# Four GNN layers on one core: two of four column blocks turned by VectorE, and a drain for the last pairs of the first three layers

## The chip, the cores and the metric

One core of a Trainium2 chip runs the whole program in one launch. The metric is the device time in microseconds. Everything is fp32.

## The reference, cut to what matters

There are 32 batches of 512 nodes with 64 features and one 512 x 512 adjacency matrix. Four layers are applied, each to `relu(layernorm(x))` and added to `x`:

```python
x = x + (h @ Ws + adj @ h @ Wn + bias)                      # layer 0
x = x + relu(adj @ relu(adj @ h @ W0) @ W1)                 # layer 1
x = x + elu(gat(h))                                         # layer 2: masked softmax attention
def gat_layer(x, graph, W, b):                              # layer 3
    h = x @ W
    s = einsum('bnd,bmd->bnm', h, h) * graph
    s = where(s == 0.0, -1e16, s)
    return einsum('bnm,bmd->bnd', softmax(s, axis=2), h) + b
cat = leaky_relu(concat of 8 heads of gat_layer, 0.01)
x = x + leaky_relu(gat_layer(cat, graph, W_out, b_out), 0.01)
```

Layer 3 has 8 heads per batch and one output layer per batch, so 9 x 32 softmaxes of 512 x 512.

## The kernel before, in words

The order of the work on PE (TensorE), DVE (VectorE) and ACT (ScalarE) is written out by hand: both stages run inside a manual schedule, in which those three engines take their instructions in program order. The queues of SP and POOL, which issue the DMAs, are ordered by the scheduler.

**Stage 1, layers 0 to 2.** The batches go in 16 pairs (M = 16). `slot(k, more)` (L1020) is one step of a software pipeline: in step k pair k is in layer 0, pair k-1 in the layer norm before layer 1, pair k-2 in the first half of layer 1, pair k-3 in its second half (`project(..., "po1b")`, L1051), pair k-4 in the preparation of layer 2 (`Gat.flip`, `prepare`, `weigh`) and pair k-5 in its scores, values and end (`Gat.scores`, L954: eight score products a pair on VectorE, L958; `values`, L963: 128 matmuls, L971; `end`, L978: the division by the sums, the exponential for elu, the two additions to x, and the centring for the next layer norm). The loop runs 21 steps, k = 0 to 20 (L1147), so that the last five steps have fewer and fewer pairs in them. Step 19 also takes the last pair's scores and values (L1103). `more` is a piece of set-up work for one step: `judge_rows(c)` (L193), six VectorE operations on one block of rows of the adjacency matrix, comes in steps 16 to 19, `judge` (L220), which gathers their verdict, in step 20. After step 17 the first steps of the attention pipeline, which have no scores yet, are put in (`flow_slot`, L1151): they make the normalized input of the first batch (`hn`, `hs`, `hx`).

**Stage 2, layer 3.** The work is cut into 144 units: 128 of two heads of one batch (`Heads`) and 16 of the output layer of two batches (`Out`). Each unit has C = 4 blocks of 128 rows, and a new unit begins every four slots of `planned` (L690). In its slots 0 to 3 a unit's scores for one block of rows (r) are reduced by VectorE and exponentiated by ScalarE: `scores` (L387, issued on PE one slot earlier into one of two PSUM buffers), `soft` (L363: on VectorE the masked row maximum, L378, for each of the two heads; on ScalarE the exponential, L371). The scores of slot k can be issued only when the buffer of two slots before has been read.

The weighted sum needs the probabilities transposed, in four blocks of 128 columns (j = 0 to 3), called column blocks below.
- Blocks 0, 1 and 2 take `transpose(j)` (L422), in slots 5, 6 and 7: 16 transposes of 64 x 64 on PE into two PSUM tiles, and two copies to SBUF. Both copies are on ScalarE (L436, L438), but for j = 1 the second is on VectorE (L441), after that slot's reductions.
- Block 3 takes `turn(r)` (L397) and `route` (L411). In slots 2 to 5, after that slot's reductions, VectorE transposes 32 x 32 blocks of the last 128 columns of both heads (L401, 128 x 256). After every second one POOL issues a write of 256 KB to a tile in DRAM (L406). In slot 5 `route` issues four reads of 128 KB (L415), two on SP, two on POOL, that put the blocks into the tile `turned`, of which there are two buffers.

`values(j)` (L443) multiplies in slots 6 to 9, one column block a slot, in PE's queue in order: block 3 in two halves of the columns, because of the order in which `turned` holds them. In slot 5 `recips` (L458) takes the reciprocals of the sums, writes them to DRAM by four small DMAs (L468, `rec_row`) and reads them back spread over the partitions by two (L473, `recb`), all six on SP. In slot 9 `normalize` (L480) multiplies by `recb` on VectorE; then follow the product with the head's weights (L565, `y_ps`), its bias on ScalarE and the leaky relu on VectorE. During eight slots of each nine units, the `Out` products (L604, `gT_ps`) are also on PE. A slot is called led when it begins with such a weight product; in a led slot the transposes come after the other PE work.

Of the kernel before, what the change touches and what calls it, by code (L numbers as in the profile page):

```python
# [8 lines left out]
F32 = mybir.dt.float32  # L9
AF = mybir.ActivationFunctionType  # L10
OP = mybir.AluOpType
# [11 lines left out]
def fast_form(  # L23
# [32 lines left out]
    Q = P // 32  # L56

# [256 lines left out]
    class Pair:  # L314
# [82 lines left out]
        def turn(self, r):  # L397
            if r == 0:
                self.turns = wk.tile([P, Q, C // 2, 2, 2, 32], F32, name="turn")
                self.rows = dram.tile([P, Q, C // 2, P], F32, name="turn_row")  # L400
            nc.vector.transpose(  # L401
                self.turns[:, :, r // 2, :, r % 2].rearrange("p a k i -> p k a i"),
                self.p[:, :, r, N - P :].rearrange("p k (a i) -> p k a i", i=32),
            )
            if r % 2:
                nc.gpsimd.dma_start(  # L406
                    self.rows[:, :, r // 2],
                    self.turns[:, :, r // 2].rearrange("p a k r i -> p a (k r i)"),
                )

        def route(self):  # L411
            rows = self.rows.rearrange("(b i) a g x -> a i b (g x)", b=Q)
            pt = wk.tile([P, Q, C // 2, 2, 2, 32], F32, name="turned")
            for a in range(Q):
                (nc.sync if a % 2 else nc.gpsimd).dma_start(  # L415
                    pt[a * 32 : (a + 1) * 32].rearrange("p b g k r i -> p b (g k r i)"), rows[a]
                )
            self.pts[C - 1] = [
                pt[:, :, :, k].rearrange("p b g r i -> p g r b i") for k in range(2)
            ]  # L420

        def transpose(self, j):  # L422
# [14 lines left out]
            if j != 1:  # L437
                nc.scalar.copy(pth[:, :, :, 1, :], ps[1])  # L438
                return None

            return lambda: nc.vector.tensor_copy(pth[:, :, :, 1, :], ps[1])  # L441

        def values(self, j):  # L443
# [3 lines left out]
            for k in range(2):  # L447

                parts = 2 if j == C - 1 and len(pt[k].shape) > 2 else 1
# [240 lines left out]
    def planned(units, products):  # L690
# [15 lines left out]
        def slot(k):  # L706
# [12 lines left out]
            copies = []  # L719

            def transposes():
                for u, j in at(k, TR, C - 1):
                    copies.append(u.transpose(j))
# [32 lines left out]
            for copy in copies:  # L756
                if copy:
                    copy()
# [43 lines left out]
    with (  # L802
# [105 lines left out]
        class Gat:  # L908
# [54 lines left out]
            def values(self):  # L963

                self.acc = [
                    ps_g.tile([P, C, F + 1], F32, name="acc") for k in range(2)
                ]
                for r in range(C):
# [9 lines left out]
            def end(self):  # L978
                rec = tiny.tile([P, 2, C], F32, name="rec")
                self.sq = o = work.tile([P, 2, C, F], F32, name="o")  # L980
                for k in range(2):
# [4 lines left out]
                    )  # L986
                e = row_pair("e")[:, 0].rearrange("p (k c f) -> p k c f", k=2, c=C)
# [31 lines left out]

        def slot(k, more):  # L1020
# [28 lines left out]
            if k - 3 in nt1b:  # L1049

                po = project([(nt1b.pop(k - 3), wl2[1])], "po1b")  # L1051
                x4 = pair_of(k - 3)
                for i in range(2):
                    nc.vector.scalar_tensor_tensor(
                        x4[:, i], po[:, :, i, :], 0.0, x4[:, i], op0=OP.max, op1=OP.add
                    )
# [14 lines left out]
            if l1:  # L1071
                po = project([(nt1, wl2[0])], "po1a")
                z = work.tile([P, C, F2], F32, name="z")
                nc.scalar.activation(z, po.rearrange("p c b f -> p c (b f)"), AF.Relu)
# [27 lines left out]

            last = gat.pop(M - 1) if k - 4 == M - 1 else None  # L1103
            if last:
                last.scores(0)
                last.scores(1)
# [631 lines left out]
```

## Time and profile before

| what | us |
|---|---|
| median of three runs (2257.47 to 2261.6) | 2259.0 |
| the profiled execution | 2259.57 |
| its span, first to last instruction | 2257.6 |
| PE busy | 2167.4 |
| DVE busy | 1748.1 |
| ACT busy | 1634.1 |
| POOL busy | 399.4 |
| the first scores of stage 2 begin | 455.96 |

Busy times are of the whole span; the two stages are different, so the shares of each are read from a table by windows. Matmul instructions overlap, so the time that PE needs for a group is the distance from its start to the start of the next group, not the length that its row shows. One fp32 matmul of the program shows as two instructions. In a timeline row the columns are start, length, engine, line, operation, tiles and count, and in brackets how long the engine had been idle and what ended that.

### The profile page before, as it was taken

Reading aid. Unit: us, or ns where it says so; the run is one execution under the profiler, and the core shown is the slowest. Engines: PE = TensorE matmul, PEld = TensorE weight load, DVE = VectorE, ACT = ScalarE, POOL = GpSimd, SP = SyncE. Lnnn points to the kernel's source line nnn. Section 1 sums busy time; section 2 is a strip of 40 time slices with the busy share of each in tenths; the row PEclk is TensorE's granted clock in tenths of the full one; section 3 lists DMA queues with packets and bytes.
Section 4 is the critical chain, followed back from the end, with each engine's and each line's share of the span. In section 5 each row is a group of like instructions: output and inputs, shape, how many; then the busy total and the mean of one; then the engine's idle time right before and its main releaser. Section 6 shows DMA issues by size and latency. Waiting matters only on the chain.

```text
span 2257.6 us, 47717 instructions
## 1 busy us (share of the span) xinstructions
PE 2167.4 (96%) x17338; PEld 1028.7 (46%) x17338; DVE 1748.1 (77%) x4542; ACT 1634.1 (72%) x3818; POOL 399.4 (18%) x616
## 2 busy tenths in 40 slices
PE   7999999789999999999999999999999999999997
PEld 4677666634444444444444434344444444444443
DVE  6788888777777787878787777777878787878785
ACT  3444443288888888888888888787878787878785
POOL 2000000012221212222222212222212122112221
PEclk9999999699999999999999999999999999999999
DMA  4000000023333333333333333333333333333333
GB/s 129 1 1 1 1 1 1 1 88 110 104 116 106 118 105 112 108 110 112 109 109 113 109 109 113 104 113 104 114 108 111 106 118 102 110 99 114 101 116 105
DMA packets 122979, 204.03 MB, mean 90 GB/s; under 512 B 29752, under 2 KB 76000, under 8 KB 122608
## 3 DMA queue, kind: packets, MB, share of 16 engines
q0 software_dynamic: 37376, 113.49, 16.5%
q1 hardware_dynamic: 85360, 87.42, 13.0%
q8 instruction: 139, 2.28, 0.4%
q14 instruction: 104, 0.85, 0.1%
HBM read 119.48 MB, written 80.28 MB: 88 GB/s over the span
## 4 chain that ended last, share of the span: by engine, by line
PE 59%; DVE 16%; issue 3%; DMA 1%; ACT 1%; SPq 0%; POOL 0%; DVEq 0%; POOLq 0%; ACTq 0%
PE s_ps L392 19%; PE av L452 18%; PE pt_ps L430 8%; DVE s_att L378 8%; PE y_ps L565 5%; PE gT_ps L604 5%; DVE pt_att L441 3%; PE g_ps L547 2%; DVE hs L518 1%; DVE turn L401 1%; DVE cat L312 1%; DVE hn L514 1%; DVE hn L513 0%; DVE least L522 0%; DVE least_out L625 0%
## 5 line engine op out<-in xcount | busy, mean ns | idle before, releaser
L371 ACT ACTIVATE p_att<-s_att,negmax 128x512 f32<-128x512 f32 x1152 | 827.0, 726 | 1.8 <-DVE negmax L378 0.8
L378 DVE CUSTOM_DVE_ANT_0 s_att<-s_ps,flow_neg 128x512 f32<-128x512 f32 x1152 | 736.4, 675 | 2.9 <-PE s_ps L392 2.9
L392 PE MATMUL s_ps<-hx,g 64*128 64x512 f32 x2048 | 573.1, 637 | 26.7 <-DVE negmax L378 23.1
L452 PE MATMUL av<-pt_att,hn 128*64 128x512 f32 x1536 | 414.2, 618 | 0.4 <-DVE rec L463 0.4
L406 POOL DMA_DIRECT2D turn_row<-turn x288 | 206.3, 716 | 1167.7 <-DVE turn L401 972.8
L430 PEld LDWEIGHTS pt_ps<-ident,p_att 64*128 64x128 f32 x6912 | 279.6, 138 | 280.6 <-issue 180.0
L436 ACT COPY pt_att<-pt_ps 128x512 f32<-128x512 f32 x432 | 250.6, 580 | 90.4 <-PE pt_ps L430 88.7
L430 PE MATMUL pt_ps<-ident,p_att 64*128 64x64 f32 x6912 | 312.6, 226 | 1.3 <-ACT pt_att L436 0.6
L392 PEld LDWEIGHTS s_ps<-hx,g 64*128 64x128 f32 x2048 | 155.7, 186 | 283.7 <-DVE negmax L378 132.0
L401 DVE STREAM_TRANSPOSE turn<-p_att 128x256 f32<-128x256 f32 x576 | 253.8, 441 | 18.1 <-ACT p_att L371 17.6
L573 ACT ACTIVATE cat<-y_ps,bh 128x512 f32<-128x512 f32 x256 | 162.0, 684 | 130.1 <-PE y_ps L565 130.1
L482 DVE TENSOR_TENSOR o_att<-av,recb 128x512 f32<-128x512 f32 x144 | 99.5, 691 | 189.2 <-PE av L452 182.7
L441 DVE COPY pt_att<-pt_ps 128x512 f32<-128x512 f32 x144 | 99.0, 687 | 180.9 <-PE pt_ps L430 180.9
L415 POOL DMA_DIRECT2D turned<-turn_row x288 | 163.1, 573 | 388.5 <-DMA turn_row<-turn 206.6
L371 ACT ACTIVATION_READ_ACCUMULATOR p_att<-s_att,negmax 128x1 f32 x1152 | 229.6, 199 | 0.0
L438 ACT COPY pt_att<-pt_ps 128x512 f32<-128x512 f32 x288 | 171.5, 596 | 0.0
L452 PEld LDWEIGHTS av<-pt_att,hn 128*64 128x64 f32 x1536 | 76.0, 134 | 194.2 <-issue 81.9
L312 DVE SCALAR_TENSOR_TENSOR cat<-cat 128x1024 f32<-128x1024 f32 x128 | 151.3, 1182 | 0.0
L452 PE MATMUL av<-turned,hn 128*64 128x256 f32 x1024 | 139.6, 392 | 0.0
L559 ACT COPY g<-g_ps 128x512 f32<-128x512 f32 x128 | 68.7, 589 | 91.5 <-PE g_ps L547 91.5
L565 PE MATMUL y_ps<-o_att,wh_sb 64*128 64x512 f32 x512 | 132.5, 594 | 0.0
L604 PE MATMUL gT_ps<-cat,wo_sb 128*64 128x512 f32 x512 | 131.9, 592 | 0.0
(174 smaller groups left out, 2148.0 us busy)
## 6 DMA issues: line engine op xcount, KB each, us to landing
turn_row<-turn POOLq DMA_DIRECT2D x288, 256.0 KB, 2.7
turned<-turn_row SPq DMA_DIRECT2D x288, 128.0 KB
turned<-turn_row POOLq DMA_DIRECT2D x288, 128.0 KB, 3.0
recb<-rec_row SPq DMA_DIRECT2D x288, 128.0 KB
rec_row<-rect SPq DMA_DIRECT2D x576, 1.0 KB
out_dram<-y SPq DMA_DIRECT2D x32, 128.0 KB
x<-in_x_dram SPq DMA_DIRECT2D x3, 1024.0 KB
x<-in_x_dram SPq DMA_DIRECT2D x4, 256.0 KB
```

The costliest lines, as they stand in the source:

```text
L312: nc.vector.scalar_tensor_tensor(t, t, 0.01, t, op0=OP.mult, op1=OP.max)
L371: nc.scalar.activation(self.p[:, k, r, :], ns[:, k], AF.Exp, bias=self.negmax[:, k, r : r + 1], scale=-1.0, accum_out=self.sum[:, k, r : r ...
L378: nc.vector.tensor_tensor_reduce(out=ns[:, k], in0=ps[:, k], in1=flow_neg[:, r], scale=-1.0, scalar=BIG, op0=OP.add, op1=OP.min, accum_out ...
L392: nc.tensor.matmul(ps[:, k], lhsT=g[halves(k), r * P : (r + 1) * P], rhs=x[halves(k), :], start=True, stop=True,)
L401: nc.vector.transpose(self.turns[:, :, r // 2, :, r % 2].rearrange("p a k i -> p k a i"), self.p[:, :, r, N - P :].rearrange("p k (a i) -> ...
L406: nc.gpsimd.dma_start(self.rows[:, :, r // 2], self.turns[:, :, r // 2].rearrange("p a k r i -> p a (k r i)"),)
L430: nc.tensor.transpose(ps[half][:, k, r], self.p[halves(half), k, r, j * P : (j + 1) * P], ident[halves(half), halves(half)],)
L436: nc.scalar.copy(pth[:, :, :, 0, :], ps[0])
L438: nc.scalar.copy(pth[:, :, :, 1, :], ps[1])
L452: nc.tensor.matmul(self.av[halves(k), g * n : (g + 1) * n], lhsT=self.v(k, j), rhs=pt[k][:, g] if parts > 1 else pt[k], start=(j == 0), st ...
L565: nc.tensor.matmul(ps, lhsT=wh_sb[halves(k), h, :], rhs=self.o[halves(k), :], start=True, stop=True,)
L604: nc.tensor.matmul(self.gps[halves(k), :], lhsT=wo_sb[:, h, :], rhs=Heads.cat[b + k, h], start=(h == 0), stop=(h == H - 1),)
```

## The change

**In stage 2** the last two column blocks (T = 2), blocks 2 and 3, take the way through `turn` and `route`; PE transposes only blocks 0 and 1, and both of their evacuations are on ScalarE. A `turn` is now 128 x 512. There are two DRAM tiles, one for each block, thus two writes after every second `turn` (four a unit) and eight reads a unit, again half on SP and half on POOL. The tile `turn` holds two blocks of rows of both column blocks and is taken anew for each two; the tiles `turned0` and `turned1` have one buffer each. The SBUF that they take is the same. `values(2)` now also goes in two halves.

**In stage 1** the loop stops after step 16 (17 steps), and `drain()` writes out by hand what the last four steps did, for the pairs 12 to 15: `g2`, `g1`, `g0` and `last`. `Gat.values` can be issued in two halves, `Gat.end` is split into `read` (takes the result out of PSUM) and `rest` (exponential, additions, centring), and `fill(n)` issues n matmuls of 128 x 512 whose result nobody reads. The layer norms' last square roots are taken together at the end of the drain. `judge_rows` moves to steps 6, 8, 10 and 12, `judge` to step 15, and the first steps of the attention pipeline go into the drain.

```diff
+    T = C // 2
...
         def turn(self, r):
+            if r % 2 == 0:
+                self.turns = wk.tile([P, T * Q, 2, 2, 32], F32, name="turn")
             if r == 0:
-                self.turns = wk.tile([P, Q, C // 2, 2, 2, 32], F32, name="turn")
-                self.rows = dram.tile([P, Q, C // 2, P], F32, name="turn_row")
+                self.rows = [
+                    dram.tile([P, Q, C // 2, P], F32, name=f"turn_row{j}") for j in range(T)
+                ]
             nc.vector.transpose(
-                self.turns[:, :, r // 2, :, r % 2].rearrange("p a k i -> p k a i"),
-                self.p[:, :, r, N - P :].rearrange("p k (a i) -> p k a i", i=32),
+                self.turns[:, :, :, r % 2].rearrange("p a k i -> p k a i"),
+                self.p[:, :, r, N - T * P :].rearrange("p k (a i) -> p k a i", i=32),
             )
             if r % 2:
-                nc.gpsimd.dma_start(
-                    self.rows[:, :, r // 2],
-                    self.turns[:, :, r // 2].rearrange("p a k r i -> p a (k r i)"),
-                )
+                for j in range(T):
+                    nc.gpsimd.dma_start(
+                        self.rows[j][:, :, r // 2],
+                        self.turns[:, j * Q : (j + 1) * Q].rearrange(
+                            "p a k r i -> p a (k r i)"
+                        ),
+                    )
 
         def route(self):
-            rows = self.rows.rearrange("(b i) a g x -> a i b (g x)", b=Q)
-            pt = wk.tile([P, Q, C // 2, 2, 2, 32], F32, name="turned")
-            for a in range(Q):
-                (nc.sync if a % 2 else nc.gpsimd).dma_start(
...
+            for j in range(T):
+                rows = self.rows[j].rearrange("(b i) a g x -> a i b (g x)", b=Q)
+                pt = wk.tile([P, Q, C // 2, 2, 2, 32], F32, name=f"turned{j}", bufs=1)
+                for a in range(Q):
+                    (nc.sync if a % 2 else nc.gpsimd).dma_start(
+                        pt[a * 32 : (a + 1) * 32].rearrange("p b g k r i -> p b (g k r i)"),
+                        rows[a],
+                    )
+                self.pts[C - T + j] = [
+                    pt[:, :, :, k].rearrange("p b g r i -> p g r b i") for k in range(2)
+                ]
...
-            if j != 1:
-                nc.scalar.copy(pth[:, :, :, 1, :], ps[1])
-                return None
-
-            return lambda: nc.vector.tensor_copy(pth[:, :, :, 1, :], ps[1])
+            nc.scalar.copy(pth[:, :, :, 1, :], ps[1])
...
-                parts = 2 if j == C - 1 and len(pt[k].shape) > 2 else 1
+                parts = 2 if j >= C - T and len(pt[k].shape) > 2 else 1
...
-                for u, j in at(k, TR, C - 1):
-                    copies.append(u.transpose(j))
+                for u, j in at(k, TR, C - T):
+                    u.transpose(j)
...
+        def fill(n):
+            p = ps_t.tile([P, N], F32, name="fill_ps", tag="ps")
+            for i in range(n):
+                nc.tensor.matmul(p, lhsT=ident, rhs=adj_t[:, 0, :], start=True, stop=True)
+
+        def drain():
+            g2, g1, g0 = gat.pop(M - 4), Gat(M - 3, n2.pop(M - 3).h), None
+            nt1b[M - 2] = copied(nt1b[M - 2], "nt1b")
+            h = n1.pop(M - 1).h
+            nt1 = copied(neighbours(lambda c: h[:, c]), "nt1")
+            g1.flip()
+            g2.scores(0)
+            ends(M - 2)
+            n = make(n2, M - 2)
+            n.a()
+            n.square()
+            g2.scores(1)
+            z = middle(nt1)
+            g1.prepare()
+            nt1b[M - 1] = neighbours(lambda c: z[:, c, :])
+            s = Spread()
+            s.add(n)
+            u = ended.pop()
+            s.add(u)
+            s.root()
+            nt1b[M - 1] = copied(nt1b[M - 1], "nt1b")
+            g2.values(range(C // 2))
+            g1.weigh()
+            s.turn()
+            n.relu()
+            flow_stats[u.i] = u.mean, u.rstd
+            g0 = Gat(M - 2, n2.pop(M - 2).h)
+            ends(M - 1)
+            n = make(n2, M - 1)
+            n.a()
+            n.square()
+            g2.values(range(C // 2, C))
+            g1.scores(0)
+            g0.flip()
+            g2.read()
+            g1.scores(1)
+            g0.prepare()
+            fill(3)
+            s = Spread()
+            s.add(n)
+            s.root()
+            g1.values()
+            s.turn()
+            n.relu()
+            last = Gat(M - 1, n2.pop(M - 1).h)
+            last.flip()
+            g0.weigh()
+            g2.rest()
+            g0.scores(0)
+            g1.read()
+            last.prepare()
+            g0.scores(1)
+            fill(6)
+            g0.values()
+            last.weigh()
+            g1.rest()
+            last.scores(0)
+            s = Spread()
+            s.add(g2)
+            for i in range(-3 * C, -1):
+                flow_slot(i)
+            g0.read()
+            last.scores(1)
+            fill(3)
+            last.values()
+            g0.rest()
+            s.add(g1)
+            last.read()
+            last.rest()
+            fill(6)
+            s.add(g0)
+            s.add(last)
+            s.root()
+            s.turn()
+            for n in (g2, g1, g0, last):
+                flow_stats[n.i] = n.mean, n.rstd
...
-                M + 4: judge,
             }
             for c in range(C):
-                begun[M + c] = lambda c=c: judge_rows(c)
-            for k in range(M + 5):
+                begun[6 + 2 * c] = lambda c=c: judge_rows(c)
+            begun[7 + 2 * C] = judge
+            for k in range(M + 1):
                 slot(k, begun.get(k))
-                if k == M + 1:
-                    for i in range(-3 * C, -1):
-                        flow_slot(i)
+            drain()
```

`ends` is the second half of layer 1 for one pair (the `po1b` product and its two VectorE additions), `middle` its first half (the `po1a` product and its relu), both as they stood in `slot`.

## The prediction, made before the changed kernel was run

> **What bounds the kernel now.** I read the granted clock and the window table first, then the chain of waits in the long stage, then the timeline of one stretch. In the window table the columns are length, busy time of PE, PEld, DVE, ACT and POOL (instructions in brackets), clock, DMA share, GB/s.
>
> ```profile
> 369.50:456.00 86.50, 63.11 (x685) 50.64 (x683) 67.19 (x130) 25.47 (x48) 0.00 (x0) 0.76 0.00 1
> 434.00:456.00 22.00, 14.83 (x131) 14.33 (x131) 9.34 (x21) 4.11 (x6) 0.00 (x0) 0.50 0.00 1
> 1300.00:1500.00 200.00, 195.74 (x1524) 81.93 (x1524) 154.28 (x420) 161.83 (x388) 40.37 (x63) 1.00 0.35 105
> ```
>
> The first three layers end in a tail of 86.5 us (369.5 to 456) in which no engine is full and the clock falls to 0.50. The attention stage after it has PE 98%, ACT 81%, DVE 77% and full clock. Its 144 units start 12.38 us apart: the reciprocal of L463 runs once a unit, first at 467.7, last at 2237.9, over 143 steps. The chain from 500 to 2200 us, by line:
>
> ```profile
> by line: PE s_ps L392 24.5%; PE av L452 23.4%; PE pt_ps L430 10.8%; DVE s_att L378 10.2%; PE y_ps L565 6.3%; PE gT_ps L604 6.2%; issue 4.0%; DVE pt_att L441 3.6%; PE g_ps L547 3.0%; DVE hs L518 1.2%; DVE turn L401 1.2%; DVE cat L312 0.8%; D
> ```
>
> About three quarters of it are PE and about 18% DVE: PE is the bound, broken by stretches in which scores wait until VectorE has freed their two PSUM buffers. What the third column block (j=2) costs PE is seen in the timeline, in a slot with its transposes (the second group, its L430) and one without:
>
> ```profile
> 1351.79 1.13 PE L392 MATMUL s_ps<-hx,g 64*128 64x512 f32 x4
> 1352.84 1.08 PE L452 MATMUL av<-pt_att,hn 128*64 128x512 f32 x4
> ...
> 1373.16 1.08 PE L392 MATMUL s_ps<-hx,g 64*128 64x512 f32 x4
> 1374.07 0.83 PE L430 MATMUL pt_ps<-ident,p_att 64*128 64x64 f32 x16
> 1374.83 1.08 PE L452 MATMUL av<-pt_att,hn 128*64 128x512 f32 x4
> ```
>
> From scores to values it is 1.05 us without and 1.67 us with the 16 transposes: they cost 0.62 us.
>
> **The route through DRAM now**, one unit, in the same timeline:
>
> ```profile
> 1303.78 0.45 DVE L401 STREAM_TRANSPOSE turn<-p_att 128x256 f32<-128x256 f32 x1
> ...
> 1304.52 0.71 POOL L406 DMA_DIRECT2D turn_row<-turn  x1 [3.53 <-DVE turn L401]
> ...
> 1307.32 0.33 SPq L415 DMA_DIRECT2D turned<-turn_row  x1
> 1307.69 1.33 SPq L468 DMA_DIRECT2D rec_row<-rect  x4
> ...
> 1308.66 0.69 DVE L441 COPY pt_att<-pt_ps 128x512 f32<-128x512 f32 x1 [1.00 <-PE pt_ps L430]
> ...
> 1309.07 0.32 SPq L415 DMA_DIRECT2D turned<-turn_row  x1
> ...
> 1311.37 1.10 SPq L473 DMA_DIRECT2D recb<-rec_row  x2
> ...
> 1316.94 1.09 PE L452 MATMUL av<-turned,hn 128*64 128x256 f32 x8
> ```
>
> The last transpose ends at 1304.23, the last read goes out at 1309.07 and lands about 3 us later (median 3.0 us in the page's DMA rows), and values(3) begins at 1316.94. So almost 5 us are spare now.
>
> [...] the trace before cannot show what twice the traffic does. [...] 441 ns for 256 columns (L401), 212 ns for 32 (L465), 1.02 ns a column. [...]
>
> **The change part by part, attention stage, per unit.**
> (a) 16 transposes leave PE: -0.62 us. Values(2) from the turned tile runs in halves like values(3); eight halves take 1.02 us from start to start (1316.94 to 1317.96), four whole ones 1.01: nothing.
> (b) The second evacuation of j=1 goes from VectorE to ScalarE. PE's next slot now has only scores (0.97) between these transposes and values(1), which needs both copies. Two ScalarE copies in a row end 1.06 us after the first starts (580 and 596 ns, second 0.46 to 0.48 after the first), and some 0.1 to 0.2 us pass before and after: +0.30 us on PE. Ends: 0, and +0.65 if ScalarE is inside an exponential (0.7).
> (c) VectorE loses that 0.69 us copy and its wait for PE (175.9 us over 137 units, 1.28 each); what follows it in its queue, the score reduction that frees PSUM, moves up. Its share of the chain is 3.6% of 12.38: -0.45 us. Ends: 0 and -0.9.
> (d) Four transposes of 512 columns instead of 256: 4 x 0.264 = +1.06 us on VectorE. Behind each are the next reductions, for which PE waits. Only the 18% in which VectorE carries the chain counts: +0.19. Ends: 0 and +0.4 (1.06 less the copy).
> (e) ScalarE loses one copy net (0.58); not on the chain: 0.
> (f) The DMAs. POOL gets 4 writes and 4 reads instead of 2 and 2, 4 x 0.72 + 4 x 0.57 = 5.2 us of its queue per unit, with waits still under 12. SP gets 4 reads instead of 2. In the built order of the new kernel, 109 of 144 units queue on SP: read of block 2, four rec_row writes, read of block 2, read of block 3, two recb reads, and only then the last read of block 3. recb waits for rec_row (2.35 us after its last issue), so that read waits too. From the end of the last transpose, with the spacing of the fence: write out at 0.29, landed and first SP read at 3.09, rec_row 3.46 to 4.79, recb 2.35 later at 7.14, done at 8.24, the last read then, 3.3 to land (median 3.0 on POOL; estimate) and 0.24 to PE: L = 11.8 us. VectorE's work from values(3) of one unit to the transpose that feeds the values(3) two units later is 1.0 (values) + 0.69 + 0.36 + 4 x 1.22 + 4 x 0.63 + 1.1 = 10.55. The loop spans two units, so a unit of the heads can't be shorter than (10.55 + 11.8)/2 = 11.2 us. Two head units take 23.98 now (1301.00 to 1324.98), 12.0 each. With (a) to (d) they would come to about 11.4: the route just fits. More traffic (the 16 engines' share was 0.35; turned and turn_row are most of it) can lengthen L: I take +0.10. Ends: 0 and +0.7.
> Sum: -0.62 + 0.30 - 0.45 + 0.19 + 0.10 = -0.48 us; 144 units: -69 us. By busy sums no engine is over: head unit PE 10.7, VectorE 10.0, ScalarE 9.7.
>
> **The drain.** It starts where slot 17 did (369.5). I walked its order with the durations of before. VectorE's parts: 32 score products (21.7 us in the tail), four reads and rests (4.1 each), two layer norms, weighing, variances, hx: about 54, which is the 67.2 above less three judge_rows of 4. PE: four values of 7.4, two neighbours of 3.5, projections, flips, prepares: 46, plus 18 filling matmuls of 0.86, 15.5. In order: the first values half at 11.5, g2 done at 20, g1's values 25.6 to 33, g0's 41 to 49 (held some 3 by a fill), the last 53 to 60, its read and rest to 65, root and turn to 67. First reduction of the attention stage at 67 instead of 88.5 (458.08), at full clock: -20 us. Ends -26 and -8; no loss, since none of its work is new but the fills.
> The judge_rows go to slots 6 to 12, where VectorE idles 1.8 us waiting for values and PE has about 10 us queued: +2, ends 0 and +6. The kernel's own end shows one more exposed block of reads: +2.
>
> **Sum.** 2257.6 - 69 - 20 + 2 + 2 = 2172.6 span; the profiled execution's 2259.6 lies 2.0 over its span, and 0.6 over the median: **2174 us**.
>
> **Rivals.**
> 1. *PE flows free*: (b) and (d) hide, VectorE stops holding PE: -0.95 a unit, -137: 2106. For: busy sums; against: ScalarE's serial pair. Chance 0.15.
> 2. *The turned blocks come late, mildly*: L = 13, head unit 11.8; the two units in nine with gT products gain 0.3. (7 x 0.2 + 2 x 0.3)/9 = 0.22, -32, with the drain: 2211. For: landings up to 5.2 us in the trace; against: median 2.7 to 3.0. Chance 0.20.
> 3. *Slower*: the same loop with heavy contention. It decides from 144 x 7/9 x (T - 12.0) = 16 + 10, T = 12.23, L = 13.9, that is 2.1 us more over three hops (write, rec_row, read). At L = 15, T = 12.8: +90 - 26: 2323. For: DMA share nearly doubling; against: even then a third of the 16 engines' time is free. Chance 0.07.
> 4. *It doesn't do what it says*: ScalarE or VectorE coupling eats (a) and the drain gains little: within 0.2%, 0.03.
> My forecast: 0.55, own range 2140 to 2205. Within 0.2% (4.5 us) is about what a measurement of this kernel can't tell from none. Faster 0.90, same 0.03, slower 0.07. The range 2110 to 2225 leaves out rival 3, the worse part of 2, the better of 1.
>
> **What would show it.** L430 at 4608 transposes; L401's successor at about 705 ns; unit period about 11.9; first attention scores near 436 with clock 1.0 before them; PE's wait for turned small. A PE wait on turned_row reads of a microsecond a unit means rival 2 or 3. A period under 11.6 means 1. A clock of 0.5 in the drain would make the drain's step wrong.

## The result, and the profile after

The kernel after takes **2330.5 us** (median of four runs, 2322.23 to 2339.44) beside 2258.4 before on the same chip: ratio 1.0306, 95% interval 1.0282 to 1.0331. It is 72 us slower; 2174 was forecast. The profiled execution took 2339.44, with a span of 2337.6.

First the window table after, for the drain and for the long stage (columns as before: length, busy time of PE, PEld, DVE, ACT, POOL, clock, DMA share, GB/s):

```profile
369.50:456.00 86.50, 82.56 (x790) 58.44 (x788) 57.20 (x116) 22.75 (x47) 0.00 (x0) 0.90 0.01 1
422.50:437.00 14.50, 13.83 (x109) 11.80 (x109) 12.11 (x24) 1.22 (x2) 0.00 (x0) 0.51 0.01 1
1300.00:1500.00 200.00, 178.51 (x1256) 73.75 (x1253) 155.76 (x393) 148.10 (x359) 80.23 (x126) 0.98 0.65 190
```

In the long stage PE has fallen from 195.74 us busy in 200 to 178.51, while DVE stays where it was and the DMA share goes from 0.35 to 0.65: no engine is full any more. The first stretch holds fills, so its busy PE says little; half clock is still there (0.51 from 422.5 to 437). The first score reduction of the attention stage begins at 455.1 instead of 458.1, and the units are 12.94 us apart (mean distance of their reciprocals, here and below) instead of 12.38. So in the two profiled executions, which are 80 us apart, stage 1 gave 3 us, and the 144 units lost 0.56 each, some 80 us, where 0.48 of gain was forecast.

The chain of waits from 500 to 2200 us, by line, and the wait table of the same stretch (engine, line, releaser: us in total, times, longest):

```profile
by line: PE av L457 16.3%; DMA turned<-turn_row 14.0%; PE s_ps L393 12.5%; DMA rec_row<-rect 8.3%; PE gT_ps L609 5.7%; DVE s_att L379 5.4%; issue 4.0%; SPq L478 3.5%; PE y_ps L570 3.3%; PE pt_ps L439 3.2%; SPq L473 3.1%; DMA turn_row<-turn 
```
```profile
DVE o_att L487 <- PE av L457: 287.2, 129, 6.3
PEld av L457 <- issue: 259.9, 246, 3.1
...
PEld av L457 <- ACT pt_att L446: 148.2, 120, 1.4
...
PE av L457 <- DMA turned<-turn_row: 106.7, 86, 2.6
```

Before, hardly a DMA stood in the chain; now the landing of `turned` has 14% and rec_row's 8%, and PE stands still 86 times in some 131 units until a turned block is there, 0.8 us a unit. The prediction had named a microsecond a unit as the sign of its rivals 2 and 3. One route in the timeline:

```profile
1307.34 0.71 DVE L405 STREAM_TRANSPOSE turn<-p_att 128x512 f32<-128x512 f32 x1
...
1308.34 1.45 POOL L411 DMA_DIRECT2D turn_row<-turn  x2 [3.32 <-DVE turn L405]
...
1311.56 1.60 SPq L473 DMA_DIRECT2D rec_row<-rect  x4
...
1313.20 0.88 SPq L423 DMA_DIRECT2D turned<-turn_row  x2
...
1315.39 1.09 SPq L478 DMA_DIRECT2D recb<-rec_row  x2
...
1316.52 5.77 SPq L423 DMA_DIRECT2D turned<-turn_row  x2
...
1320.73 1.09 PE L457 MATMUL av<-turned,gV 128*64 128x256 f32 x8 [1.70 <-DMA turned<-turn_row]
```

The last transpose ends at 1308.05 and values(3) begins at 1320.73, after 1.70 us of waiting: 12.7 us. The last read goes out right behind the recb reads, at 1316.5 (the first of the two in that row; the second belongs to the next unit), and needs another 4.1 us to land. The landing times of GpSimd's DMAs, in the page's last part, have grown from 2.7 (writes) and 3.0 (reads):

```profile
turn_row<-turn POOLq DMA_DIRECT2D x576, 256.0 KB, 3.3
...
turned<-turn_row POOLq DMA_DIRECT2D x576, 128.0 KB, 3.5
```

### The profile page after: what moved, and what is told of

Same layout as the page of the kernel before. It is cut to its first block, busy times and chain, and to the rows that moved or that the text cites. A ratio compares the mean times of both kernels' runs of the same rounds, so it can differ in the third digit from the quotient of the medians.

```text
span 2337.6 us, 45886 instructions
## 1 busy us (share of the span) xinstructions
PE 2122.6 (91%) x15646; PEld 995.1 (43%) x15646; DVE 1808.4 (77%) x4397; ACT 1559.4 (67%) x3671; POOL 769.3 (33%) x1192
## 4 chain that ended last, share of the span: by engine, by line
PE 52%; DMA 21%; DVE 11%; ACT 7%; SPq 6%; issue 3%; DVEq 0%; ACTq 0%
PE av L457 13%; DMA turned<-turn_row 11%; PE s_ps L393 10%; PE nt_ps L880 7%; DMA rec_row<-rect 7%; PE acc L972 5%; DVE s_att L379 4%; PE gT_ps L609 4%; SPq L478 3%; SPq L473 3%; PE pt_ps L439 3%; PE y_ps L570 2%; DMA turn_row<-turn 2%; DVE turn L405 2%; ACT pt_att L445 2%
## 5 line engine op out<-in xcount | busy, mean ns | idle before, releaser
L411 POOL DMA_DIRECT2D turn_row<-turn x576 | 419.1, 762 | 936.4 <-DVE turn L405 746.5
L405 DVE STREAM_TRANSPOSE turn<-p_att 128x512 f32<-128x512 f32 x576 | 407.2, 707 | 52.6 <-ACT p_att L372 51.5
L423 POOL DMA_DIRECT2D turned<-turn_row x576 | 320.3, 562 | 327.6 <-PE y_ps L570 84.4
L457 PE MATMUL av<-turned,hn 128*64 128x256 f32 x2048 | 283.7, 395 | 108.4 <-DMA turned<-turn_row 107.9
L457 PE MATMUL av<-pt_att,hn 128*64 128x512 f32 x1024 | 276.2, 618 | 46.9 <-ACT pt_att L446 46.8
L445 ACT COPY pt_att<-pt_ps 128x512 f32<-128x512 f32 x288 | 167.5, 582 | 152.5 <-PE pt_ps L439 151.6
L439 PEld LDWEIGHTS pt_ps<-ident,p_att 64*128 64x128 f32 x4608 | 181.4, 139 | 190.0 <-issue 150.0
L457 PEld LDWEIGHTS av<-turned,hn 128*64 128x64 f32 x2048 | 138.9, 137 | 247.0 <-issue 213.9
L439 PE MATMUL pt_ps<-ident,p_att 64*128 64x64 f32 x4608 | 198.8, 226 | 1.1 <-ACT pt_att L445 0.6
L446 ACT COPY pt_att<-pt_ps 128x512 f32<-128x512 f32 x288 | 171.6, 596 | 0.0
L972 PE MATMUL acc<-v,s 64*128 64x65 f32 x2048 | 124.1, 280 | 0.7 <-DVE s L958 0.4
```

What stands on the lines that cost most here:

```text
L405: nc.vector.transpose(self.turns[:, :, :, r % 2].rearrange("p a k i -> p k a i"), self.p[:, :, r, N - T * P :].rearrange("p k (a i) -> p k ...
L411: nc.gpsimd.dma_start(self.rows[j][:, :, r // 2], self.turns[:, j * Q : (j + 1) * Q].rearrange("p a k r i -> p a (k r i)"),)
L423: (nc.sync if a % 2 else nc.gpsimd).dma_start(pt[a * 32 : (a + 1) * 32].rearrange("p b g k r i -> p b (g k r i)"), rows[a],)
L439: nc.tensor.transpose(ps[half][:, k, r], self.p[halves(half), k, r, j * P : (j + 1) * P], ident[halves(half), halves(half)],)
L445: nc.scalar.copy(pth[:, :, :, 0, :], ps[0])
L457: nc.tensor.matmul(self.av[halves(k), g * n : (g + 1) * n], lhsT=self.v(k, j), rhs=pt[k][:, g] if parts > 1 else pt[k], start=(j == 0), st ...
```

## Experiments

My theory after the result: the route of the turned blocks is too late for PE, and its latency, not the engines' work, sets the unit. Rivals: the added traffic as such, the single buffers of `turned0` and `turned1`, the wider work of VectorE, and the half clock. "Before" ran beside all of these, at 2260 to 2263 us.

**The stage alone.** The diff of stage 2 on top of the kernel before; stage 1 keeps its loop and judges:

```diff
-            for k in range(M + 1):
+            for k in range(M + 5):
...
-            drain()
```

> The first three layers as before, the attention stage as after. In the trace of the changed kernel the first score reduction of the attention stage stands at 455.1 us against 458.1 before, so the drain would have brought only 3 us, and the attention stage alone would have cost some 75 to 80 us: 2335 us expected. If the drain brought the 20 us that were forecast and something else was lost, this kernel would be near 2350.

2319.8 us, ratio 1.0261 (1.0228 to 1.0294), unit period 12.76.

**The drain alone**, the other half of the diff, with the attention stage of before:

> The drain and the moved judge steps, with the attention stage as before. By the changed kernel's trace 3 us less than before: about 2255 us. If the drain works as forecast (20 us) 2240; if its place only looks worse because of the new attention stage, also 2240.

2255.7 us, ratio 0.9975 (0.9967 to 0.9984). The two ratios make 1.0236 together, the kernel after has 1.0306. The 0.7% between (16 us) is not explained; in the profiled executions it lies in the attention stage, whose units are 12.94 us apart in the kernel after and 12.76 in the stage alone, with the same code there.

**Nobody waits for the route.** The stage alone, with all DMAs going out, but the values of blocks 2 and 3 taken from a constant:

```diff
         def values(self, j):
             pt = self.pts.pop(j)
+            if j >= C - T:
+                pt = [urow.rearrange("p (b g r i) -> p g r b i", b=Q, g=2, r=2)] * 2
```

> Attention stage as after, but values of blocks 2 and 3 are multiplied from a constant tile (the outer scale row) instead of from the turned tiles; every transpose, write and read still goes out, but nothing waits for the reads: this leaves out the use of blocks 2 and 3. If the lateness of the route is the whole loss, the time falls below before, to between 2150 (PE flows free) and 2200 us (the forecast's sum without its DMA term, about 2190). If the coupling of ScalarE's two serial copies and of VectorE's longer transposes is the loss, it stays above 2300.

2228.2 us, ratio 0.9848 (0.9826 to 0.9871), period 12.11. Waiting for turned blocks costs 2319.8 - 2228.2 = 92 us, more than the whole loss; but the time stays some 40 us above the forecast's sum, so the wait is not the only thing that the forecast missed. What makes the blocks late? In the stage alone, the chain from 500 to 2200 us (133 units) has 57 landings of `turned`; 53 of them follow a landing of rec_row, and 36 end this circle, shown once round in the chain of the stage alone (start, length, what):

```profile
1311.07 1.10 PE av L457 x8
...
1312.20 0.69 DVE o_att L487
1312.89 0.12 DVE rec L468
...
1314.26 2.47 DMA rec_row<-rect
...
1316.81 0.45 SPq L478
...
1317.32 0.59 SPq L478
...
1317.95 4.97 DMA turned<-turn_row
1322.92 0.25 issue
1323.16 1.10 PE av L457 x8
```

values(3) lets VectorE do o_att (the product with recb in `normalize`); only behind it, in VectorE's queue, stands the reciprocal of the next unit; its rec_row must land before SP can issue recb (the two SPq rows); and behind recb stands the last read, for the next values(3). This circle closes within one unit; the 36 have a median of 12.8 us from values(3) to values(3), just the unit period of 12.76. In the other units of the stretch the chain takes other ways, through PE's work for the most part.

**Block 2's reads on SP, block 3's on POOL**, so that the block needed last never stands behind recb:

```diff
-                    (nc.sync if a % 2 else nc.gpsimd).dma_start(
+                    (nc.gpsimd if j else nc.sync).dma_start(
```

> Attention stage as after, but the four reads of block 2 are all on SP and the four of block 3 all on POOL, so that no read stands behind the recb reads. If the queue order makes the last read late (it goes out 8.5 us after the last transpose), the route shortens by about 3 us and the time falls to about 2200 us. If it is contention of the transfers (the same bytes in the same time), it stays within 20 us of the stage-2-only kernel, above 2300.

2567.9 us, ratio 1.1348 (1.1316 to 1.138): a miss. The wait table of this run from 500 to 2200 us shows a new circle:

```profile
POOL turned L423 <- PE av L457: 261.6, 44, 7.9
```

POOL's read into `turned1` waits until PE has read the unit before, up to 7.9 us, and the next unit's writes stand behind it in POOL's queue. (That queue's order is seen in the kernel after: at 1314.98 a write goes out right behind two reads, 0.93 us after its transpose; at 1308.34, with no read ahead of it, 0.29.) The run says nothing on recb, since it made another queue block.

**Two buffers for `turned1`** ask whether such waits already hold the plain order (the normalised output goes over `recb`, for room):

```diff
-                pt = wk.tile([P, Q, C // 2, 2, 2, 32], F32, name=f"turned{j}", bufs=1)
+                pt = wk.tile([P, Q, C // 2, 2, 2, 32], F32, name=f"turned{j}", bufs=1 + j)
...
-            self.o = wk.tile([P, N], F32, name="o_att")
+            self.o = self.recb
```

> The stage of the kernel after alone, with two buffers for the turned tile of block 3 instead of one (room is made by writing the normalised output over recb). If reads are held because TensorE has not yet read the one buffer of the unit before, and hold the writes behind them on GpSimd's queue: 2250 to 2290, and the wait of the turned reads for TensorE's values is gone. If the reads are late by queue order and landing alone: 2310 to 2325.

2323.1 us, 1.0261 (1.023 to 1.0291), the same as with one: the single buffer of block 3 is not the cause. The one of block 2 was not tried.

**All turned reads ahead of the reciprocals**:

```diff
-                u.recips()
                 u.route()
+                u.recips()
```

> The stage of the kernel after alone (2320 us by itself) with the route emitted ahead of the reciprocals: all four reads of SyncE's queue now stand ahead of the rec_row writes and recb reads, no buffer and no traffic changes. If the last read is late because it queues behind recb (median 8.5 us after the last transpose): it leaves about 3 us sooner, and the time falls to 2260 to 2285, unless recb is then late itself. If the reads are late for their landing times or for their buffers: 2310 to 2325, the last read leaves sooner but values(3) does not start sooner.

2343.3 us, 1.0357 (1.0326 to 1.0388). It is slower than either expectation. SP's last read leaves 4.91 us after the last transpose in the median, no longer 8.36, but the first recb read goes from 7.6 to 10.3: DVE's o_att now waits for recb (189.6 us in 1700). With both on SP one of the two is late.

**recb issued by POOL**, behind its reads, so that no read of a turned block stands behind it and SP's queue no longer waits for rec_row:

```diff
-                nc.sync.dma_start(
+                nc.gpsimd.dma_start(
                     self.recb[halves(k), :],
```

> The stage of the kernel after alone (2320 us) with the two recb reads issued by GpSimd instead of SyncE, behind its four turned reads: no read of a turned block stands behind a wait for rec_row any more, and recb is not put later. If the late read of block 3 is late because it queues behind recb (in the chain of waits of the stage alone, 53 of 57 waits for a turned read follow rec_row, recb and then the read): the loop from values(3) over o_att, rec, rec_row, recb and the read is cut, and the time falls to 2235 to 2275. If landing times under traffic are the cause and not the order: 2310 to 2330.

2288.2 us, 1.0115 (1.0097 to 1.0132). That is between the two expectations. The queue order is worth 32 of the 92 us, net of what the move adds to POOL's queue. PE's wait shrinks by half, in the wait table from 500 to 2200 us of this run:

```profile
PE av L457 <- DMA turned<-turn_row: 50.7, 45, 2.7
```

In the stage alone it is 95.2 us in 88 waits.

**Values one slot later**, about 3 us more of slack, with the order of the queues as the scheduler then makes it:

```diff
-    VA = TR + 1
+    VA = TR + 2
...
-            pt = pbuf.tile([P, 2, N], F32, name="pt_att", bufs=2)
+            pt = pbuf.tile([P, 2, N], F32, name="pt_att", bufs=3)
...
-            self.o = wk.tile([P, N], F32, name="o_att")
+            self.o = self.recb
```

> The stage of the kernel after alone (2320 us) with the values of every block one slot later (about 3 us more between the last transpose and values(3)), three buffers for pt_att, and the normalised output over recb to make room. If the route's latency against the order of the stage is what the 92 us are: the wait of TensorE for turned nearly goes, and the time comes to 2225 to 2245, the level of the run without any wait for the route. If queues and landings stretch with whatever slack there is, or if the transposed blocks or recb are then late: above 2290.

2257.3 us (2243.6 to 2264.4), 0.9978 (0.9965 to 0.9992): in this kernel the product of head 6 of the second batch of each pair is taken one slot ahead of that head's leaky relu, so a part of the computation is changed. The run takes back 62 of the 92 us, fewer than expected: PE still waits 82.7 us for turned, with the mean landing in the chain at 5.7 us. And slack is not all that it changes. A slot later, o_att comes behind the next unit's reciprocal in VectorE's queue and no longer ahead of it, so the circle is cut too: in the chain of the stage alone the reciprocal follows o_att directly 47 times, here never, and the first recb read leaves 3.9 us after the last transpose instead of 7.6. Slack and cut were not tried apart. POOL's reads wait longer for PE to free the single buffers, 94.1 us against 48.6 in the stage alone; that was not tried apart either.

**The traffic alone.** The kernel before, with a second write of each turned pair and a second set of reads that nobody uses (the normalised output goes over `recb` here too, for room):

```diff
+                nc.gpsimd.dma_start(
+                    self.idle[:, :, r // 2],
+                    self.turns[:, :, r // 2].rearrange("p a k r i -> p a (k r i)"),
+                )
...
+                (nc.sync if a % 2 else nc.gpsimd).dma_start(
+                    it[a * 32 : (a + 1) * 32].rearrange("p b g k r i -> p b (g k r i)"), rows[a]
+                )
```

> The kernel before, with a second write of each turned pair to another DRAM tile and a second set of four reads into a tile that nobody uses, on the same queues: the DMA traffic and the queue entries of the kernel after, the computation of the kernel before (the normalised output goes over recb to make room). If contention of the traffic makes the route late, TensorE waits for turned here too: 2300 or more. If the traffic only lengthens landings by about half a microsecond each, the 4.8 us that are spare before take it: 2258 to 2270.

2282.4 us, 1.0094 (1.0074 to 1.0114): between the two expectations. Traffic costs 22 us here by itself.

**Half the bytes, as many DMAs**, on the run in which nobody waits for the route (only the lower 64 partitions are written, only their halves read):

```diff
-                        self.rows[j][:, :, r // 2],
+                        self.rows[j][: P // 2, :, r // 2],
...
-                        rows[a],
+                        rows[a, :, : Q // 2],
```

> As the run without any wait for the route (2228 us; values of blocks 2 and 3 multiply a constant tile, so the output is not the reference's), with as many writes and reads, each of half the bytes (the upper half of the partitions stays out of the route). Without block 2's traffic it was 2197. If the bytes cost these 31 us: 2208 to 2216. If the number of DMAs in the queues does, 2225 to 2230.

2196.1 us, 0.9709 (0.9692 to 0.9725), below either expectation: all 32 us come back with as many DMAs in the queues (POOL is busy with them for 645.6 us in 1700, against 719.1). It is the bytes, not the number. What they delay is recb, as the wait tables from 500 to 2200 us show, first with the full traffic, then with the half:

```profile
DVE o_att L489 <- DMA recb<-rec_row: 69.3, 36, 3.4
```
```profile
DVE o_att L489 <- DMA recb<-rec_row: 12.2, 6, 4.1
```

The scheduler also put recb a read earlier on SP with the half traffic, in 32 of the 144 units. This is not the cause: with the full traffic o_att never waited for recb in those 32, and in the 112 with the same order its waits fall from 38 (77.0 us, whole run) to 6 (12.2).

**Without block 2's traffic, wide turn**, and then **with the narrow turn**. Both start from the run without the wait; the first drops the writes and reads of block 2, the second also takes 256 columns:

```diff
-                for j in range(T):
+                for j in range(1, T):
```
```diff
-                self.p[:, :, r, N - T * P :].rearrange("p k (a i) -> p k a i", i=32),
+                self.p[:, :, r, N - P :].rearrange("p k (a i) -> p k a i", i=32),
```

> As the run without any wait for the route (2228 us; values of blocks 2 and 3 multiply a constant tile, so the output is not the reference's), and without the writes and reads of block 2: the wide turn with the traffic of the kernel before. If the added traffic and queue entries cost the 0.12 to 0.15 us a unit that they cost in the kernel before: 2207 to 2212. If VectorE's wide turn alone sets it: 2225 to 2230.

> As the run with the wide turn and the traffic of the kernel before, but with a turn of 256 columns: it lacks both the wide turn and block 2's traffic and route. By the prediction's steps (a), (b), (c), -0.77 us a unit: 2150. By its step (d) it is only 0.19 us a unit, 27 us, under the wide turn. If the wide turn costs more, 0.4 to 0.6 us a unit, as VectorE sets the pace in more places than its share of the chain before: 60 to 90 us under it, 2130 to 2150.

2196.9 us, 0.9714 (0.9697 to 0.973), and 2196.4 us, 0.9716 (0.97 to 0.9733): the first below what was expected, the second far above. The traffic costs 31 us again. The wide turn costs **nothing**: VectorE is busy 1409 us of 1700 with it and 1275 without, and PE does not notice. And steps (a), (b) and (c) together give 65 us, not 111. The window from 500 to 2200 us of the kernel before, then of the run with the narrow turn, and PE's wait for the copies in the wait table of the latter:

```profile
500.00:2200.00 1700.00, 1667.31 (x12994) 696.44 (x12992) 1319.26 (x3604) 1385.82 (x3325) 352.16 (x549) 1.00 0.36 110
```
```profile
500.00:2200.00 1700.00, 1621.37 (x11623) 660.60 (x11619) 1274.66 (x3549) 1347.27 (x3251) 360.86 (x562) 1.00 0.38 113
```
```profile
PE av L459 <- ACT pt_att L446: 52.6, 127, 0.6
```

Per unit (12.38 and 11.92 us apart, 137.3 and 142.6 units) PE is busy 12.14 and 11.37 us and idle 0.24 and 0.55. Of the 0.55, 52.6/142.6 = 0.37 are the wait for the second of two serial copies.

**Steps (b) and (c) by themselves**: in the kernel before, the second copy of block 1 on ScalarE; and the other way round, back on VectorE, in the run without the wait for the route:

```diff
-            if j != 1:
-                nc.scalar.copy(pth[:, :, :, 1, :], ps[1])
-                return None
-
-            return lambda: nc.vector.tensor_copy(pth[:, :, :, 1, :], ps[1])
+            nc.scalar.copy(pth[:, :, :, 1, :], ps[1])
```

> The kernel before with one edit: the second copy of block 1 on ScalarE, as in the kernel after; steps (b) and (c) alone. By the prediction -0.15 us a unit: 2238. With VectorE as loaded as in the kernel after it was -0.40 us a unit (58 us); here VectorE has the narrow turn and TensorE is 98% busy, so a gain of at most the 33 us in 1700 that TensorE idles, 2215, and if TensorE is the bound already, no gain: 2255 to 2275.

> The run without any wait for the route (values of blocks 2 and 3 multiply a constant tile, so that the output is not the reference's; 2228 us), with the second copy of block 1 on VectorE again as before. By the prediction's steps (b) and (c), +0.15 us a unit for taking them back: 2250. If instead the two serial ScalarE copies hold values(1) by more than the step had (the trace shows some 1.1 us a unit of TensorE waiting for ScalarE's pt_att): 2190 to 2215.

2252.0 us, 0.9957 (0.9941 to 0.9974): 10 us of gain, 0.07 a unit. And 2286.1 us, 1.0112 (1.0088 to 1.0136), 58 us over 2228.2: where the turn is wide, the same copy on VectorE costs 0.40 a unit.

**The drain with two things moved.**

```diff
-            begun[7 + 2 * C] = judge
...
-            last.flip()
             g0.weigh()
             g2.rest()
+            last.flip()
...
             last.scores(1)
+            judge()
             fill(3)
```

> The drain alone with the attention stage of before (2255.7 us, 0.9975 of before), with two moves: judge, whose VectorE reduction waits 8.7 us for own_ps in the last full slot, goes between the last scores and the last values; and the rest of g2, whose exponential stands on ScalarE behind the copy of last's flip, ahead of that flip. If these two waits are why the drain gained 3 to 5 us and not 20: 2240 to 2247. If the half clock in it is the cause: 2252 to 2256.

2243.4 us, 0.9916 (0.99 to 0.9933): 12 us under the drain as it was. Two waits of VectorE in the drain alone are gone, and with them the half clock. First the wait table of the drain alone, from 345 to 450 us, then the window of the drain alone, then that of the mended one:

```profile
DVE x L1000 <- ACT e L996: 9.3, 2, 8.3
...
DVE unsound L225 <- PE own_ps L224: 8.7, 1, 8.7
```
```profile
345.00:450.00 105.00, 98.43 (x946) 71.44 (x945) 70.19 (x143) 28.53 (x58) 0.00 (x0) 0.89 0.01 1
```
```profile
345.00:450.00 105.00, 98.50 (x1004) 68.06 (x1004) 81.49 (x174) 37.44 (x76) 0.75 (x1) 1.00 0.01 1
```

In the same 105 us VectorE does 81.5 us of work instead of 70.2, at clock 1.00 instead of 0.89. The first score reduction begins at 442.5 instead of 454.6, so the last 7 us of the stretch, and the work in them, already belong to the attention stage.

**Versions.** The mended drain with the ScalarE copy in the stage of before:

> Both parts that gained by themselves: the drain with judge and g2's rest moved (2243 us) and the second copy of block 1 on ScalarE in the attention stage of before (10 us less by itself). If they add up, as they lie in different stages: 2231 to 2236. If the stage starts so much sooner that the gain of one is taken by the other, as the drain and the new stage were 15 us more together than apart: 2240 to 2248.

2233.8 us, 0.9879 (0.9859 to 0.9898): the gains add. The kernel after with late values and the mended drain, the output units one unit later:

```diff
-            due.append(((b + 1, 2), b - 1))
+            due.append(((b + 1, 3), b - 1))
```

> The kernel after with what the runs suggest: values one slot later (the output units one unit later too, so that the product of the last heads still follows their leaky ReLU), three buffers for pt_att, the normalised output over recb, and the drain with judge and g2's rest moved. The stage alone with late values was 2257 and the drain's two moves were worth 12 to 17: 2238 to 2250. If the drain and the stage disturb one another as in the kernel after, 15 us more: 2255 to 2265.

2212.9 us, 0.9788 (0.976 to 0.9817), better than either expectation. One product of the last output unit still came ahead of its leaky relu; with it in its place:

```diff
-            h = off + 2 * C + 2
+            h = off + 2 * C + 2 - (b == B - 2)
```

> The kernel of late_full (2212.9 us) with the last output unit's products one slot later, so that the product of head 6 of the last image follows its leaky ReLU there too: nothing else is moved. As that is one slot in some 650: 2211 to 2219, the fastest of all kernels here. If the wait of the last unit for its own products stretches the end of the kernel by a slot: 2216 to 2222.

**2218.0 us** (2210.6 to 2230.1), ratio 0.9793 (0.9772 to 0.9815): the whole change, mended, beats the kernel before by 2.1% and the kernel after by 5%. It is some 22 us better than the stage with late values (2257) and the drain's 17 us make together; the shift of the output units by a unit is the only other difference, and what it does was not tried by itself.

## Why the prediction was wrong

The forecast sum was -0.48 us a unit; the ladder of runs gives +0.41 for the stage alone (59 us):

| step | forecast, us a unit | measured | from |
|---|---|---|---|
| (a)+(b)+(c) | -0.77 | -0.45 | narrow turn, no wait: 65 us |
| (d) wider turn | +0.19 | 0.00 | wide against narrow: 0.5 us |
| (f) traffic, nobody waiting | none of its own | +0.22 | 31 us |
| (f) waiting for the route | +0.10 in all | +0.64 | 92 us |

- **(f) failed, and decided the sign.** The sum took the wrong path. It let the reciprocal start with the transposes; in VectorE's queue it stands behind o_att, which waits for values(3). So there is a shorter circle, in one unit and not over two, that the sum hadn't. In the chain shown it is 12.1 us (4.97 of them the landing; with the forecast 3.3 it would be 10.4, and would not bind), in the median 12.8, against a unit of 12.76 in the stage alone. The loop over two units, which the sum did have, was also short: the last read, which leaves at 8.4 (8.24 in my sum), lands in 4.1 behind two recb reads and not in 3.3, and in a tenth of the units it leaves after 9.9. With 8.4 + 4.1 + 0.24 for the route and VectorE's 10.6, which the quickest tenth needs, this loop comes to an estimated 11.7 us a unit, so by itself it did not set the 12.76. (The measured distances on it can't decide that: from the last transpose to values(3) it is 13.64 us on average, from there to the transpose two units on 11.85, and their sum is two units in every kernel, also in the one before, with 12.46 and 12.25, waits of all kinds included.) "The route just fits" had no margin for either.
- **Traffic** was counted only as latency of the route. It cost 31 us with nobody waiting for the route, at least in part through recb, which I had not followed: the wait for it goes from 6.2 us (narrow) or 21.1 (wide, without block 2's traffic) to 69.3. So with twice the turned bytes, whose writes and half of whose reads are on POOL's queue, o_att waits longer for recb, which SP issues, at a mean share of only 0.67 (0.38 without block 2's traffic).
- **(a) right, (c) oversized.** PE's busy time fell 0.77 a unit, a little more than (a)'s 0.62. But (c) was to bring 0.45 by sparing PE waits, when PE's whole idle time was 0.24 a unit: VectorE's share of the chain had counted time in which PE worked too. (b) was 0.30 and PE waits 0.37.
- **(d)** counted what VectorE has to do; with its copy gone it had the room, and the cost is nothing. The 264 ns that it took for 256 more columns were my estimate; 707 less 441 give 266. With the copy kept it was 0.40 a unit (with all the traffic going): steps (c) and (d) are one budget, and the copy and the wider turn could not be priced apart.
- **The unit period** forecast at 11.9 would have held only without the wait: 11.92 to 12.11. The turn of 707 ns and 4608 transposes are as forecast.
- **The drain** forecast 20 us and gave 3 (5 by itself). Costed at the engines' sums, it left out two waits by order: judge, moved to step 15, holds VectorE 8.7 us until PE comes to its transpose, and has no term in my sum, whose 2 us are for the judge_rows; and g2's exponential stands on ScalarE behind a copy that waits for PE (8.3). With both moved, 17 us come and the clock is 1.00 from 345 to 450 us, with the same 18 fills as in the drain alone at 0.89: the full clock of the forecast was an assumption, and what the fills do for it was not shown. The half clock that the prediction named as its sign of failure comes after these waits, which the kernel after has too: there VectorE waits until 351.60 and until 413.67, and the clock is 0.56 from 357 to 364 us, 1.00 from 400 to 422 and 0.52 from 422 to 439. Both were moved together, so the share of each is open, and so is how the waits bring the half clock about.
- **Rival 3** named the outcome and part of the reason. Contention is there (31 us, and a landing of 4.1 for 3.3), but the larger part is the wait, of which 32 us go with recb's place in the queue. That the kernel after comes near its L of 13.9 (13.96 on average) proves nothing, as that distance includes waits of all kinds. I gave it 0.07 because a third of the 16 engines' time would still be free; that share said nothing of DMAs in series behind one queue: at 0.65 in the kernel after, the last read of the route shown left SP 8.5 us after the last transpose, right behind recb.

Open: the 16 us by which the parts are better apart than together, and how much of the rest of the wait (60 us after recb's move) is landing time, how much POOL's order and how much the single buffers.

## What to carry to other kernels

A transfer that was hidden with 5 us to spare isn't free when it is doubled (31 us here with nobody waiting for it, and 92 for the wait): follow its whole circle, through every queue in which it stands behind something else, to the instruction that waits for it and back, and compare its length with the period you hope for, not with the present one. A gain from sparing a wait can't exceed the idle time of the engine that sets the pace (0.45 us a unit forecast here, 0.24 idle). And when a route is late, try the consumer a slot later (here for one buffer) before giving up the idea: it gives slack, and it can also take an instruction out of the circle, as it did here with the reciprocal.

## What the runs showed of the hardware

In this kernel the landing times of the DMAs grew while the mean share of the 16 engines stayed at 0.73 or less: POOL's reads of 128 KB take a median of 3.0 us at a DMA share of 0.36 (before), 3.5 at 0.64 (after), and 4.4 in the last, mended kernel at 0.73; the writes of 256 KB 2.7, 3.3 and 3.7. The half-size ones, as many as after (share 0.43), take 2.3 and 2.6. The last kernel's DMAs, first:

```profile
turn_row<-turn POOLq DMA_DIRECT2D x576, 256.0 KB, 3.7
...
turned<-turn_row POOLq DMA_DIRECT2D x576, 128.0 KB, 4.4
```

But the mean share did not tell which transfer is slow. In the run of the traffic alone, at a share of 0.65, the reads that go out first stay at 3.0 us, as before, and those issued behind them take 3.8 (the writes 2.9 and 3.4):

```profile
turned<-turn_row POOLq DMA_DIRECT2D x288, 128.0 KB, 3.0
...
idle<-idle_row POOLq DMA_DIRECT2D x288, 128.0 KB, 3.8
```
